# The feed-forward layer's small steps, one step later in a latent-attention loop, and queued behind a copy on VectorE

## The chip, the cores and the metric

The kernel runs on one core of one Trainium2 chip. The metric is the device time of one execution in microseconds. Of several executions the median counts: 2151.29 us before the change, over three runs (2148.95 to 2156.46).

On this core five engines work in parallel, each on its own queue of instructions, in the order in which they stand there: TensorE (PE in the profile) multiplies and transposes, VectorE (DVE) and ScalarE (ACT) do elementwise work and copies, GpSimd (POOL) does some elementwise work as well, SyncE (SP) starts transfers. An engine that waits for another's result holds up everything behind it on its own queue.

## The reference

x holds four sequences of 512 rows and 256 columns. A layer is four parts, each added to x; the first layer is latent attention, feed-forward, cosine attention, the same feed-forward again:

```
x = x + latent_attention(layernorm(x))
x = x + ffn(layernorm(x))
x = x + cosine_attention(layernorm(x))
x = x + ffn(layernorm(x))
```

The second layer has parts of other kinds (a gated linear attention, attention with low-rank adapters, a workspace). The change lies where the feed-forward part behind the latent attention overlaps with that attention. That part is

```
out    = (layernorm(x) @ weight) * scale
v_norm = max(norm(out), 1e-7)                   # one number for each row
out    = out * tanh(v_norm) / (v_norm + 1e-7)
o_norm = max(norm(out), 1e-7)
out    = out * min(0.99 / o_norm, 1)
```

So behind one matrix product there is a chain of operations on one number for each row (in the kernel, tiles of 128x4), and at the end one scaled addition to x. The latent attention is causal attention with 16 heads: scores = q k, softmax, probabilities times values, with rotated parts of q and k, and keys and values read through a low-rank projection.

## The kernel before, in words

x stays in the on-chip memory, one tile of 128x4x256 for each of the four sequences ("batches" b = 0 to 3): 512 rows, in four row tiles (i = 0 to 3) of 128.

The latent attention (`mla`) is one loop over steps n = 32 b + 4 g + i: batch b, pair of heads g (0 to 7), row tile i. A step issues, in this order: the scores of step n (`scores`, L390), the queries of the next pair where i = 0 (`queries`, matmuls at L238, in the loop's helper), parts of the next batch's preparation (`prepare`) (in steps 17, 19, 21 and 23 of 32), the turning of the probabilities of step n - 2 (`turn`, transposes at L417), the values of a finished pair (`values`, L429), and last the feed-forward work that is woven in at this step.

On the other engines this means, for one step: VectorE masks the scores and takes the negated row maximum (L256, `masked`, two instructions on 128 x up to 512, each with a short read of its accumulator), ScalarE takes the exponential (L397), VectorE the reciprocal of the row sums (L401), GpSimd multiplies (L402), TensorE transposes (L417), and VectorE and ScalarE in turn copy the turned probabilities from PSUM into `prt` (`evac`: L129 on VectorE, L133 on ScalarE). For the queries VectorE runs two rope products (L320, L321) and a shuffle (L323), GpSimd adds (L324), ScalarE copies the other half (L378). Scores, turned probabilities, queries and the transposes of a layernorm share three PSUM buffers of one kind ("two"). The first part of the preparation is a layernorm: statistics (L178, L179), the reciprocal root in steps L154 to L160 (`rpow`: VectorE, Ln and Exp on ScalarE, VectorE), xn (L208, four of 128x256), eight transposes (L218) and one copy on ScalarE (L219, `own_xt`).

`ffn_steps` (from L481) is a generator for the feed-forward part of one batch. It stops after the layernorm, and after its transposes; then it issues the matmuls (L238), the product with the scale (L497, 128x1024 on VectorE), four Squares with row sums (L500, ScalarE), and the small steps on 128x4: L503, `rpow` (L154 to L160), L505, L507, Tanh on ScalarE (L509), after which the table of logarithms and exponentials is loaded again (L170), L511 to L518, and the four products that add to x (L520, VectorE). The generators of batches 0, 1 and 2 are called in steps 6, 10 and 14 of the next batch, that of batch 3 in the cosine attention behind it, and a second set of the same generators runs later still, for the feed-forward part behind the cosine attention.

The order of TensorE's instructions is the order in which the program issues them (`manual_schedule`). On the other engines a scheduler decides, which plays the program through with estimated times and issues what it takes to be ready first; the program's own order breaks ties and gives the priorities. `issue_after`, which the kernel uses elsewhere (L956), gives the scheduler a further rule: what is issued inside the block stands behind a named instruction where both are on one engine's queue. It adds no wait for another engine.

Of the kernel before, what the change touches and what calls it, by code (L numbers as in the profile page):

```python
# [9 lines left out]
F32 = mybir.dt.float32  # L10
I32 = mybir.dt.int32
U32 = mybir.dt.uint32
AF = mybir.ActivationFunctionType
ALU = mybir.AluOpType
AX = mybir.AxisListType

P = 128
B = 4
T = 512
D = 256  # L20
NI = T // P
# [4 lines left out]
class Model:  # L26
# [21 lines left out]
    def pool(self, name, bufs=1, **kw):  # L48

        return self.tc.tile_pool(name=name, bufs=bufs, reuse_waits="tile", **kw)  # L50
# [73 lines left out]
    def evac(self, out, in_, scale=None):  # L124

        self.n_evac += 1
        if self.n_evac % 2:
            if scale is None:
                self.nc.vector.tensor_copy(out, in_)  # L129
            else:  # L130
                self.nc.vector.tensor_scalar_mul(out, in_, scale)
        elif scale is None:
            self.nc.scalar.copy(out, in_)  # L133
        else:
            self.nc.scalar.mul(out, in_, scale)
# [342 lines left out]
                    next(woven[n], None)  # L478


    def ffn_steps(self, b, pause=True):  # L481
        nc = self.nc
        w, s = self.ffn_w, self.ffn_s
        eps = 1e-7
        xn, xt = self.norm_tiles()
        self.layernorm(xn, self.x[b])
        p2 = self.norm
        if pause:
            yield
        self.turned(xn, xt)  # L490
        yield
        py = self.two().rearrange("p a (i d) -> p (a i) d", d=D)
        for i in range(NI):
            self.mm(py[:, i, :], [(xt[:, c, i * P : (i + 1) * P], w[:, c, :]) for c in range(NC)])
        y = p2.tile([P, NI, D], F32, name="fy", tag="fy")
        ss = self.small.tile([P, NI], F32, name="f_ss", tag="f_ss")
        nc.vector.tensor_tensor(y, py, s.unsqueeze(1).to_broadcast([P, NI, D]), op=ALU.mult)  # L497
        for i in range(NI):
            sq = p2.tile([P, D], F32, name="fsq", tag="fsq")
            nc.scalar.activation(sq, y[:, i, :], AF.Square, accum_out=ss[:, i : i + 1])  # L500

        n = self.small.tile([P, NI], F32, name="f_n", tag="f_n")
        nc.vector.tensor_scalar_max(ss, ss, 1e-30)  # L503
        self.rpow(n, ss, 1.0, 0.0, self.tmps())
        nc.vector.tensor_tensor(n, n, ss, op=ALU.mult)  # L505
        v = self.small.tile([P, NI], F32, name="f_v", tag="f_v")
        nc.vector.tensor_scalar_max(v, n, eps)  # L507
        f = self.small.tile([P, NI], F32, name="f_f", tag="f_f")
        nc.scalar.activation(f, v, AF.Tanh)  # L509
        self.logs()  # L510
        nc.vector.tensor_scalar_add(v, v, eps)  # L511
        nc.vector.reciprocal(v, v)
        nc.vector.tensor_tensor(f, f, v, op=ALU.mult)
        nc.vector.tensor_tensor(n, n, f, op=ALU.mult)
        nc.vector.tensor_scalar_max(n, n, eps)
        nc.vector.reciprocal(n, n)
        nc.vector.tensor_scalar(n, n, 0.99, 1.0, op0=ALU.mult, op1=ALU.min)
        nc.vector.tensor_tensor(f, f, n, op=ALU.mult)  # L518
        for i in range(NI):
            nc.vector.scalar_tensor_tensor(  # L520
                self.x[b][:, i, :], y[:, i, :], f[:, i : i + 1], self.x[b][:, i, :], op0=ALU.mult, op1=ALU.add
            )
        yield

    @staticmethod
# [1128 lines left out]
def emit(tc, aps):  # L1654


    with ExitStack() as ctx:
        m = Model(ctx, tc, aps)
        ctx.enter_context(tc.manual_schedule(engines={mybir.EngineType.PE}))
        pool = m.pool  # L1660
        sb = ctx.enter_context(pool("shared_b"))
        with m.norms("norm_1", xn=1, xt=1), ExitStack() as stack:
            sa = stack.enter_context(pool("shared_a"))
            with m.psum("ps_1", two=3, acc=2):

                def shared(tag):

                    kb = int(tag.strip("sab"))
                    t = (sa if kb == 16 else sb).tile([P, kb * 256], F32, name=tag, tag=tag)
                    return [t, 0]  # L1670

                ffn = [m.ffn_steps(b) for b in range(B)]
                woven = {32 * (b + 1) + n: ffn[b] for b in range(B - 1) for n in (6, 10, 14)}
                m.mla(shared, woven | {116: m.cos_first()})
                cos = m.cos_load(shared)
                gla = m.gla_load(shared)
                woven = {(0, k): ffn[B - 1] for k in range(3)}
                ffn = [m.ffn_steps(b) for b in range(B)]
                woven |= {(4 * b + 5, k): ffn[b] for b in range(B - 1) for k in (1, 2, 3)}
                prepare, run = m.gla_stage(gla)  # L1680

                def first():

                    m.gla_fold(gla)
                    yield
                    place = shared("s16a")
                    for part in (0, 1, 3, 4, 2):
                        prepare(0, part, place)
                        if part == 1:
                            with m.tc.high_priority(offset=2000):  # L1690
                                prepare(1, "norm", None)
                        if part != 3:
                            yield

                g = first()
                woven |= {at: g for at in ((15, 0), (15, 1), (15, 3), (16, 1), (16, 2))}
                m.cos(cos, woven)
            wp = ctx.enter_context(pool("late_w", side="right"))
            ws = m.ws_load(wp)
            with m.psum("ps_g", st=2, two=1, acc=2), pool("gla_w") as gp, pool("gla_3", 2) as g3, pool(  # L1700
                "gla_2", 2
            ) as g2:
                fold = m.ws_fold(ws, wp, gp)
                extra = {n: [ffn[B - 1]] for n in (1, 3, 5)} | {n: [fold] for n in (6, 9, 10, 13, 14, 15)}
                run(range(B), extra, g2, g3)
        lora = m.lora_load(wp, [shared("s8"), shared("s4a"), shared("s4b")])
        with pool("lora_1", side="right") as l1, pool("lora_w", 2) as lw, m.norms("norm_2", xn=1, xt=2):
            first, run = m.lora_stage(lora, range(B), m.lora_tiles(l1), lw)
            with m.psum("ps_2", two=2, acc=4):
                g = first()  # L1710
                m.ws(ws, ("by", "xt", "xf"), {(1, n): g for n in (1, 2, 4, 8)})
            with m.psum("ps_3", two=4), pool("lora_2", 2) as l2:
                run(l2)
        with m.psum("ps_4", two=2, acc=4):
            m.ws(ws, ("xf", "xt", "by"))
        m.store()
# [121 lines left out]
```

## Time and profile before

| | |
|---|---|
| median of three runs | 2151.29 us |
| lowest, highest | 2148.95, 2156.46 us |
| the profiled execution | 2155.31 us, its span 2153.5 us |
| granted TensorE clock, mean | 0.971 |
| TensorE busy | 1988.9 us (92%) |
| VectorE busy | 1268.0 us (59%) |
| ScalarE busy | 761.1 us (35%) |
| GpSimd busy | 577.8 us (27%) |
| latent attention | about the first 600 us of the span |
| product with the scale (L497) in it | at 229.07, 370.72 and 512.37 us |

The profile is of one execution. A busy engine is one that runs an instruction; idle time of an engine that nothing waits for costs nothing. The profile names, for each wait, the instruction that came last. The three places at which the changed part of the feed-forward layer runs follow each other at 141.65 us. The granted clock is the share of full speed at which TensorE runs; it is 1 or 0.5 at any moment, so the mean says how long it was halved.

### The profile page before, as it was taken

How to read it: one execution, taken by the hardware profiler on the slowest of the kernel's cores; microseconds unless marked ns; L12 is line 12 of the kernel's file. 1: busy time of each engine (PE TensorE's matmuls, PEld its weight loads, DVE VectorE, ACT ScalarE, POOL GpSimd, SP SyncE). 2: the span in 40 equal slices, each digit the busy share in tenths (PEclk: the TensorE clock that was granted, in tenths of full speed). 3: DMA queues.
4: the chain of work that ended last, by engine and by line, in shares of the span. 5: the costliest groups of instructions: out<-in, count | busy, mean ns of one | idle time of the engine just before them, and what ended most of it. 6: DMA issues, size and time to landing. Idle time of an engine off the chain costs nothing.

```text
span 2153.5 us, 25620 instructions
## 1 busy us (share of the span) xinstructions
PE 1988.9 (92%) x9414; PEld 1062.3 (49%) x9414; DVE 1268.0 (59%) x3185; ACT 761.1 (35%) x1696; POOL 577.8 (27%) x530
## 2 busy tenths in 40 slices
PE   7999999999899999999999999988988989899886
PEld 4546555564454454544454454523355644444454
DVE  5565655656446434653664454398955766656545
ACT  2433443434323222322232223234224334334542
POOL 2433333433302212212212221156720122212100
PEclk9999999999999999999999999988899999999898
DMA  5020000000000000000000000010000000000001
GB/s 177 1 91 1 1 1 1 1 1 1 20 1 0 0 1 0 0 1 0 0 1 0 1 0 0 1 46 0 1 25 1 1 1 1 1 1 1 1 1 40
DMA packets 19837, 22.87 MB, mean 11 GB/s; under 512 B 4832, under 2 KB 17664, under 8 KB 19328
## 3 DMA queue, kind: packets, MB, share of 16 engines
q1 hardware_dynamic: 19712, 21.24, 3.0%
q8 instruction: 74, 1.21, 0.2%
q14 instruction: 51, 0.42, 0.1%
HBM read 19.14 MB, written 2.10 MB: 10 GB/s over the span
## 4 chain that ended last, share of the span: by engine, by line
PE 62%; DVE 16%; issue 11%; ACT 6%; POOL 4%; DMA 1%; SPq 0%; POOLq 0%; DVEq 0%; ACTq 0%
PE ps_two L238 26%; PE ps_acc L238 11%; PE ps_two L390 5%; PE ps_acc L429 3%; PE ps_two L1508 3%; DVE ps_two L256 3%; PE ps_two L417 2%; POOL e L687 2%; PE ps_two L1551 2%; DVE gs L888 2%; PE ps_acc L1249 1%; PE ps_two L654 1%; DVE ln_st L178 1%; ACT prob L397 1%; PE ps_acc L645 1%
## 5 line engine op out<-in xcount | busy, mean ns | idle before, releaser
L687 POOL TENSOR_TENSOR e<-e 128x1024 f32<-128x1024 f32 x64 | 150.7, 2355 | 619.4 <-ACT e L679 592.2
L256 DVE CUSTOM_DVE_ANT_0 ps_two<-ps_two,mask 128x256 f32<-128x256 f32 (+3 forms) x512 | 249.7, 503 | 74.3 <-PE ps_two L390 40.7
L679 ACT ACTIVATE e<-ps_two 128x1024 f32<-128x1024 f32 x128 | 130.8, 1023 | 346.8 <-PE ps_two L238 346.6
L238 PE MATMUL ps_acc<-e,cv 128*128 128x512 f32 x512 | 234.9, 601 | 1.4 <-DVE cot L685 0.9
L402 POOL TENSOR_TENSOR prob<-prob,psum_row 128x256 f32<-128x256 f32 (+3 forms) x128 | 159.7, 1255 | 284.6 <-DVE psum_row L401 278.4
L238 PE MATMUL ps_two<-cq,ckt 128*128 128x512 f32 x512 | 230.5, 593 | 3.0 <-DVE cq L656 3.0
L397 ACT ACTIVATE prob<-ps_two,nmax 128x128 f32<-128x128 f32 (+3 forms) x256 | 132.5, 526 | 148.6 <-DVE nmax L256 139.4
L238 PEld LDWEIGHTS ps_acc<-e,cv 128*128 128x128 f32 x512 | 93.5, 190 | 138.3 <-issue 116.0
L238 PEld LDWEIGHTS ps_two<-cq,ckt 128*128 128x128 f32 x512 | 96.6, 190 | 116.9 <-issue 114.8
L238 PE MATMUL ps_two<-own_xt,s 128*128 128x512 f32 x200 | 108.7, 675 | 13.9 <-DVE prt L129 11.1
L238 PE MATMUL ps_two<-own_xt,s16a 128*128 128x512 f32 x256 | 114.9, 592 | 0.1
L238 PE MATMUL ps_two<-s16b,cot 128*128 128x256 f32 x512 | 113.1, 379 | 0.0
L1540 ACT ACTIVATE lo_ex<-ps_two 128x1024 f32<-128x1024 f32 (+3 forms) x128 | 85.3, 704 | 72.8 <-PE ps_two L1508 67.5
L390 PE MATMUL ps_two<-kvt,qx 64*128 64x256 f32 (+3 forms) x512 | 103.6, 481 | 6.1 <-ACT qx L378 2.4
L417 PEld LDWEIGHTS ps_two<-ident,prob 128*128 128x128 f32 x640 | 71.0, 142 | 74.6 <-issue 48.5
L417 PE MATMUL ps_two<-ident,prob 128*128 128x128 f32 x640 | 94.6, 279 | 14.0 <-ACT qx L378 4.5
L238 PEld LDWEIGHTS ps_two<-s16b,cot 128*128 128x128 f32 x512 | 97.3, 190 | 20.1 <-issue 7.7
L1541 POOL TENSOR_SCALAR_AFFINE_SELECT lo_ex<-lo_ex 128x256 f32<-128x256 f32 x128 | 51.7, 408 | 193.5 <-ACT lo_ex L1540 192.3
L688 DVE TENSOR_TENSOR es<-e 128x512 f32<-128x512 f32 x64 | 43.9, 687 | 95.0 <-POOL e L687 93.9
L390 PE MATMUL ps_two<-kpe,qy 64*128 64x256 f32 (+3 forms) x512 | 90.5, 430 | 0.9 <-POOL qy L324 0.9
L1508 PE MATMUL ps_two<-lo_qm,lo_t 32*128 32x128 f32 (+3 forms) x512 | 76.2, 475 | 11.6 <-ACT lo_ex L1540 5.3
L429 PE MATMUL ps_acc<-prt,kv 128*64 128x256 f32 (+3 forms) x512 | 79.0, 452 | 2.7 <-DVE prt L129 2.7
(429 smaller groups left out, 3400.9 us busy)
## 6 DMA issues: line engine op xcount, KB each, us to landing
x<-in_x SPq DMA_DIRECT2D x4, 512.0 KB, 7.7
s16b<-in_mla_wo SPq DMA_DIRECT2D x1, 2048.0 KB, 18.6
s16a<-in_cos_wq SPq DMA_DIRECT2D x1, 2048.0 KB, 9.3
s16b<-in_cos_wo SPq DMA_DIRECT2D x1, 2048.0 KB, 8.6
out_x<-x SPq DMA_DIRECT2D x4, 512.0 KB, 2.9
s16a<-in_mla_wqn SPq DMA_DIRECT2D x1, 1536.0 KB, 13.6
s<-in_mla_wqa SPq DMA_DIRECT2D x1, 1024.0 KB, 10.4
s4a<-in_mla_wkb SPq DMA_DIRECT2D x1, 512.0 KB, 7.4
```

The lines of the kernel that those rows point to most:

```text
L238: self.nc.tensor.matmul(out, lhsT=l, rhs=r, start=k == 0, stop=k == n - 1)
L256: self.nc.vector.tensor_tensor_reduce(out=sc[:, :n], in0=sc[:, :n], in1=self.mask[:, T - n :], scale=-1.0, scalar=3.0e38, op0=ALU.add, op1 ...
L390: nc.tensor.matmul(sc[:, k, :n], lhsT=q[r, rows], rhs=key[r, :n], start=first, stop=not first)
L397: nc.scalar.activation(pr[:, k, :n], sc[:, k, :n], AF.Exp, bias=nm[:, k : k + 1], scale=-1.0, accum_out=sm[:, k : k + 1],)
L402: nc.gpsimd.tensor_tensor(pr[:, :, :n], pr[:, :, :n], sm.unsqueeze(2).to_broadcast([P, 2, n]), op=ALU.mult)
L417: nc.tensor.transpose(pt[:, k, keys], pr[:, k, keys], self.ident)
L429: nc.tensor.matmul(po[k * R : (k + 1) * R, j * P :], lhsT=s.kv[:, j, 0, :], rhs=prt[:, k, j, j * P :], start=j == 0, stop=j == NI - 1,)
L679: nc.scalar.activation(t.e[:, pair * 2 : pair * 2 + 2, :], sc, AF.Exp)
L687: nc.gpsimd.tensor_tensor(e2, t.e[:, 0:2, :], t.e[:, 2:4, :], op=ALU.add)
L1508: nc.tensor.matmul(scs[k // 2][:, k % 2, : keys], lhsT=left[r, rows], rhs=right[r], start=True, stop=True)
L1540: nc.scalar.activation(ex[:, hs, :], sc[:, :, :n], AF.Exp, scale=0.25)
L1541: nc.gpsimd.affine_select(out=ex[:, hs, :P], in_=ex[:, hs, :P], compare_op=ALU.is_ge, fill=0.0, base=0, pattern=[[0, 2], [1, P]], channel_ ...
```

## The change

`evac` keeps the instruction of its latest copy on VectorE. `ffn_steps` takes a further argument, `late`. Where it is set, the generator stops once more behind the four Squares; the small steps are issued at its next call, inside `issue_after` with that latest copy, so that those of them that run on VectorE are queued behind it. `late` is set for batches 0, 1 and 2 of the first set, and their generators are called in step 15 as well. The latest copy at that moment is that of the turned probabilities of step 13. All other uses of the generator stay as they are. No instruction is added or left out. In the changed kernel the small steps L503 to L520 stand at L507 to L524, four lines further down (L501 on).

```diff
@@ evac
             if scale is None:
-                self.nc.vector.tensor_copy(out, in_)
+                self.copied = self.nc.vector.tensor_copy(out, in_)
@@ ffn_steps
-    def ffn_steps(self, b, pause=True):
+    def ffn_steps(self, b, pause=True, late=False):
...
             nc.scalar.activation(sq, y[:, i, :], AF.Square, accum_out=ss[:, i : i + 1])
-
-        n = self.small.tile([P, NI], F32, name="f_n", tag="f_n")
-        nc.vector.tensor_scalar_max(ss, ss, 1e-30)
-        self.rpow(n, ss, 1.0, 0.0, self.tmps())
...
+        if late:
+
+            yield
+        with self.tc.issue_after(self.copied.ins) if late else ExitStack():
+
+            n = self.small.tile([P, NI], F32, name="f_n", tag="f_n")
+            nc.vector.tensor_scalar_max(ss, ss, 1e-30)
+            self.rpow(n, ss, 1.0, 0.0, self.tmps())
+            nc.vector.tensor_tensor(n, n, ss, op=ALU.mult)
...
+            nc.scalar.activation(f, v, AF.Tanh)
+            self.logs()
...
+            for i in range(NI):
+                nc.vector.scalar_tensor_tensor(
+                    self.x[b][:, i, :], y[:, i, :], f[:, i : i + 1], self.x[b][:, i, :], op0=ALU.mult, op1=ALU.add
+                )
         yield
@@ emit
-                ffn = [m.ffn_steps(b) for b in range(B)]
-                woven = {32 * (b + 1) + n: ffn[b] for b in range(B - 1) for n in (6, 10, 14)}
+                ffn = [m.ffn_steps(b, late=b < B - 1) for b in range(B)]
+                woven = {32 * (b + 1) + n: ffn[b] for b in range(B - 1) for n in (6, 10, 14, 15)}
```

More of the change, by code (lines that the diff above doesn't have):

```diff
@@ L500, in ffn_steps @@
             nc.scalar.activation(sq, y[:, i, :], AF.Square, accum_out=ss[:, i : i + 1])
-        n = self.small.tile([P, NI], F32, name="f_n", tag="f_n")
-        nc.vector.tensor_scalar_max(ss, ss, 1e-30)
-        self.rpow(n, ss, 1.0, 0.0, self.tmps())
[L505 to L522, printed above, removed]
+        if late:
+            yield
@@ new lines, in ffn_steps @@
+        with self.tc.issue_after(self.copied.ins) if late else ExitStack():
[3 more added lines that the diff above has]
+            nc.vector.tensor_tensor(n, n, ss, op=ALU.mult)
+            v = self.small.tile([P, NI], F32, name="f_v", tag="f_v")
+            nc.vector.tensor_scalar_max(v, n, eps)
+            f = self.small.tile([P, NI], F32, name="f_f", tag="f_f")
+            nc.scalar.activation(f, v, AF.Tanh)
+            self.logs()
+            nc.vector.tensor_scalar_add(v, v, eps)
+            nc.vector.reciprocal(v, v)
+            nc.vector.tensor_tensor(f, f, v, op=ALU.mult)
+            nc.vector.tensor_tensor(n, n, f, op=ALU.mult)
+            nc.vector.tensor_scalar_max(n, n, eps)
+            nc.vector.reciprocal(n, n)
+            nc.vector.tensor_scalar(n, n, 0.99, 1.0, op0=ALU.mult, op1=ALU.min)
+            nc.vector.tensor_tensor(f, f, n, op=ALU.mult)
+            for i in range(NI):
+                nc.vector.scalar_tensor_tensor(
+                    self.x[b][:, i, :], y[:, i, :], f[:, i : i + 1], self.x[b][:, i, :], op0=ALU.mult, op1=ALU.add
+                )
```

## The prediction

> **What bounds the kernel now.** I read the page first: whole span, busy times, chain that ended last.
>
> ```profile
> span 2153.5 us, 25620 instructions
> PE 1988.9 (92%) x9414; PEld 1062.3 (49%) x9414; DVE 1268.0 (59%) x3185; ACT 761.1 (35%) x1696; POOL 577.8 (27%) x530
> PE 62%; DVE 16%; issue 11%; ACT 6%; POOL 4%; DMA 1%; SPq 0%; POOLq 0%; DVEq 0%; ACTq 0%
> ```
>
> TensorE is busy 92% of the span, so a change on VectorE can win only where TensorE stands still. The sum below is made against this execution: 2155.31 us, 1.8 us more than its span, and 4.0 us above the median of the runs, 2151.29. Next I asked for TensorE's waits around the first of the three places that the change touches (225 to 262 us), and for the clock of four stretches of it.
>
> ```profile
> PE ps_two L238 <- DVE prt L129: 2.0, 1, 2.0
> PE ps_acc L429 <- DVE prt L129: 1.0, 1, 1.0
> ```
>
> ```profile
> 227.47:230.88 3.41, 3.41 (x16) 1.72 (x14) 1.23 (x1) 0.52 (x3) 0.54 (x1) 1.00 0.00 0
> 230.88:234.29 3.41, 1.40 (x15) 1.04 (x13) 1.76 (x9) 2.06 (x10) 0.00 (x0) 1.00 0.00 0
> 234.29:237.71 3.42, 3.42 (x4) 1.36 (x5) 3.10 (x18) 2.37 (x9) 0.31 (x1) 0.50 0.01 2
> ```
>
> The columns are the stretch, its length, the busy time of TensorE, its weight loads, VectorE, ScalarE and GpSimd, the granted clock, DMA. The queries' matmuls (L238) wait 2.0 us for the copy of turned probabilities, the values (L429) 1.0 us for a later one. A stretch in which TensorE was busy 1.40 of 3.41 us is followed by one at half clock. At the second place the stretch from 374.24 us was busy 1.81 of 3.41 us, and the clock stayed full. Then VectorE and GpSimd in order of time.
>
> ```profile
> 229.07 1.23 DVE L497 TENSOR_TENSOR fy<-ps_two,r_ffn_s 128x1024 f32<-128x1024 f32 x1 [2.68 <-PE ps_two L238]
> 232.50 0.17 DVE L503 TENSOR_SCALAR f_ss<-f_ss 128x4 f32<-128x4 f32 x1 [2.20 <-ACT fsq L500]
> ...
> 233.46 0.68 DVE L129 COPY prt<-ps_two 128x512 f32<-128x512 f32 x1
> ...
> 242.44 0.93 DVE L518 TENSOR_TENSOR f_f<-f_f,f_n 128x4 f32<-128x4 f32 x1
> ...
> 245.22 1.21 DVE L129 COPY prt<-ps_two 128x1024 f32<-128x1024 f32 x1
> ```
>
> ```profile
> 242.08 1.27 POOL L324 TENSOR_TENSOR qy<-rope,rope 128x512 f32<-128x512 f32 x1 [2.22 <-DVE f_n L516]
> ...
> 254.33 1.89 POOL L402 TENSOR_TENSOR prob<-prob,psum_row 128x1024 f32<-128x1024 f32 x1 [3.44 <-DVE psum_row L401]
> ```
>
> ```profile
> 254.99 1.26 DVE L157 TENSOR_TENSOR rp<-rp,kvrs 128x4 f32<-128x4 f32 x1
> ```
>
> VectorE stands 2.20 us because L503 waits for the fourth Square; the mask and the copy that the queries need are behind it. That is the stall the change goes for. The other thing to see: L157 on 128x4 takes 1.26 us where GpSimd is inside a normalisation (L402), and both end together (256.25 and 256.22); elsewhere this form takes 0.16. L518 (0.93, else 0.16) ends at 243.37 with GpSimd's L324 (243.35). [...] The masks, rope and copies, which read PSUM, are not held.
>
> **The change, part by part.** Nothing is added or taken away: TensorE, GpSimd and SyncE keep their order, and no DMA moves. On VectorE and ScalarE only the three places in the latent attention move (fy at 229.07, 370.72 and 512.37); swaps of 0.1 to 0.2 us instructions in the last stage I cost at nothing, as they are neighbours in the same wait.
>
> *The wait that goes.* Scores 15 end at 230.95. One mask takes 0.61 until its successor starts, the copy 0.68: the queries can start at 232.3 instead of 234.20, 1.9 us earlier at each place. Queries 8 x 0.43 = 3.44, turn 0.66, scores 1.06: TensorE is through at 237.5.
>
> *The wait that comes.* In the new order the masks of both steps, both pairs of exponentials and the reciprocals (L401) stand ahead of L157, which they start GpSimd's normalisation before. On ScalarE: exponentials of 512 from 233.4 (1.45), Ln pair 0.2, exponentials of 128 (0.8), Exp pair 0.2: L157 can start at 235.95. GpSimd has had its reciprocal since 235.1 and runs 1.89 + 0.61 us, to 237.1 and 237.7. L157 is held to 237.1 (+1.1), L158 to 237.7 (+0.4); unheld they would take 0.15 each, and held as in the row above up to 1.26, and I take the rows, as L402 has the same shape in both. Then come rope's two (0.61 each), small ones, the shuffle (0.73), and only then the four xn (L208), the first done at 240.2. The second meets GpSimd's L324 (1.27, from 240.0) and is held to 241.4 (+0.9), the fourth ends at 242.1; before it ended at 237.18. TensorE, which next needs xn for its transposes (L218), stands from 237.5 to 240.2, 2.7 us, and is then fed one at a time to 242.9 (before 242.3). So the 1.9 us are gone again; the new wait takes their place.
>
> *Behind it.* ScalarE's Tanh waits for L507 (241.5) and reloads its table (1.28) before it copies own_xt, done at 244.4 (243.4): scores 18 at 244.5, +1.0. The copy that the values need no longer stands behind the four L520: values at 246.1, -0.4. But L520 now starts inside a normalisation (1.04 us, held 0.7) and stands ahead of the next masks of 384: these start at 249.0 instead of 246.43. Their exponentials, normalisation and turn are that much later; TensorE has scores and a key projection meanwhile, and loses 0.9 us at the next queries (before 253.97) and some at the turns after. Net +1.0 a place, against about -2.3 if the 2.4 us of holds ahead of xn were not there.
>
> *Third place.* The same start, but the layernorm of the next stage is woven in: its four second xn (4 x 0.33) and the L520 now stand ahead of the masks of step 19, so turn 18 comes after 539.19. And the copy for turn 15 waits behind the last statistics: turn 16 stands some 3 us. Net +1.2.
>
> *Clock.* The trace has no row of the new waits' clock. Lower bound: nothing, +3.2 in all. Upper: each new stretch with TensorE busy under 0.41 is followed by 3.41 us at half clock, up to 1.7 us. I take the rows' side: the stretch from 237.7 would be busy about a tenth, so 241.1 to 244.5 runs at half, doubling 1.7 us of transposes, half of which lies under the wait for own_xt: +0.9; second place +0.6; third, where the values and scores (2.4 and 1.0 us) fall into it, +1.5. The half-clock stretches of before, at places one and three, go, but cost nothing: the second place, without one, reaches its values at the same distance (388.12 less 141.65 is 246.47, against 246.49).
>
> [...]
>
> Sum: 1.0 + 1.0 + 1.2 = 3.2, and 0.9 + 0.6 + 1.5 = 3.0: +6.2 us, 2161.5 against this execution, 2157.5 against the median.
>
> [...]
>
> **Rivals.** *Faster:* the new holds don't come. If GpSimd starts its normalisation after L157 and L158 (0.3 us of work), xn is done 2.4 us sooner, TensorE hardly stands, and each place gains 2.3: -7, 2144. For it: L157 with f_n was not held in before (0.15). Against: there GpSimd was idle until 237.40. It decides once L157 and L158 start under 0.2 us after the reciprocal; I have 0.9.
>
> *No change to be measured:* the waits come, the clock stays: +3.2, 2154.5. For it: before, a half-clock stretch cost nothing at two places.
>
> *Much slower:* the masks 2.6 us late pass on whole, as there are three PSUM buffers for scores, turns and queries, and a full half-clock stretch (1.7) joins: 4.3 x 3 = +12.9, 2164. Against: TensorE has 3.7 us of work in between (scores 1.94, key projection 1.76), and its waits behind them were 0.2 us at most.
>
> **How the numbers follow.** 0.3% (6.45 us) is about what a measurement of this kernel can tell. Chances: the forecast 0.48, over the bound 0.28 of it; clock stays 0.17 (slower 0.02); faster rival 0.15, of which 0.10 over the bound, since -7 is hardly beyond it; much slower 0.20. Faster 0.10, same 0.40, slower 0.50. The range leaves out the faster rival's far end and what lies above +12.9 plus 2 us of spread: 2146 to 2166. The forecast's own is 2153 to 2161.
>
> **What would show it.** Right: no wait of the queries' L238 at the three places; L157 with f_n near 1.2 us; a wait of L218 of 2 to 3 us; half clock within 4 us behind it. Wrong: L157 at 0.16, or values more than 2 us earlier. It would be wrong above all if ScalarE runs the Exp pair ahead of the exponentials of 128, or GpSimd starts later than 235.9.

## The result and the profile after

The change makes the kernel slightly slower: 2158.46 us against 2150.22 us, medians of 22 runs each on the same chips. The ratio is 1.0031, with a 95% interval of 1.0019 to 1.0042. By the ratio that is 6.7 us (4.1 to 9.0); the medians themselves are 8.24 us apart. The forecast was 2157.5 us from a sum of +6.2.

The profiled execution of the changed kernel took 2163.61 us, 8.3 more than that of before. The page of it, span, busy times and chain:

```profile
span 2161.8 us, 25624 instructions
PE 1996.3 (92%) x9414; PEld 1068.4 (49%) x9414; DVE 1274.5 (59%) x3185; ACT 760.1 (35%) x1696; POOL 577.0 (27%) x530
PE 62%; DVE 17%; issue 11%; ACT 5%; POOL 4%; DMA 1%; SPq 0%; POOLq 0%; DVEq 0%; ACTq 0%
```

Every engine runs as many instructions as before (the 4 more of the whole count are on none of these five rows). TensorE runs the same 9414 matmuls and is busy 7.4 us longer, at a mean granted clock of 0.967 in place of 0.971. TensorE's waits at the first place (222 to 262 us) in the changed kernel:

```profile
PE ps_two L218 <- DVE xn L208: 3.5, 2, 2.6
PE ps_two L238 <- ACT prob L397: 1.0, 1, 1.0
PE ps_two L238 <- DVE prt L129: 0.2, 1, 0.2
```

The wait of the queries for the copy has gone from 2.0 to 0.2 us, and that of the values (1.0) is gone as well. In their place the layernorm's transposes (L218) wait 3.5 us in two pieces, and the next queries wait 1.0 us for a late exponential instead of 0.2. VectorE, in order of time, at that place:

```profile
229.51 1.22 DVE L497 TENSOR_TENSOR fy<-ps_two,r_ffn_s 128x1024 f32<-128x1024 f32 x1 [2.68 <-PE ps_two L238]
...
236.38 1.24 DVE L157 TENSOR_TENSOR rp<-rp,f_n 128x4 f32<-128x4 f32 x1
237.54 0.15 DVE L157 TENSOR_TENSOR rp<-rp,ln_rstd 128x4 f32<-128x4 f32 x1
237.66 0.54 DVE L158 SCALAR_TENSOR_TENSOR rp<-rp,f_n 128x4 f32<-128x4 f32 x1
...
240.28 1.66 DVE L208 TENSOR_SCALAR xn<-x,ln_mv,ln_rstd 128x256 f32<-128x256 f32 x2
241.86 0.16 DVE L511 TENSOR_SCALAR f_v<-f_n 128x4 f32<-128x4 f32 x1
241.93 0.72 DVE L208 TENSOR_SCALAR xn<-x,ln_mv,ln_rstd 128x256 f32<-128x256 f32 x2
...
247.33 1.01 DVE L522 TENSOR_TENSOR f_f<-f_f,f_n 128x4 f32<-128x4 f32 x1
248.38 1.67 DVE L524 SCALAR_TENSOR_TENSOR x<-fy,f_f,x 128x256 f32<-128x256 f32 x4
249.97 0.56 DVE L256 CUSTOM_DVE_ANT_0 ps_two<-ps_two,mask 128x384 f32<-128x384 f32 x1
```

For comparison, L157 and the first mask of 384 in the kernel before:

```profile
234.06 0.15 DVE L157 TENSOR_TENSOR rp<-rp,f_n 128x4 f32<-128x4 f32 x1
...
246.43 0.54 DVE L256 CUSTOM_DVE_ANT_0 ps_two<-ps_two,mask 128x384 f32<-128x384 f32 x1
```

And GpSimd in the changed kernel:

```profile
235.71 2.46 POOL L402 TENSOR_TENSOR prob<-prob,psum_row 128x1024 f32<-128x1024 f32 x2 [7.28 <-DVE psum_row L401]
240.52 1.27 POOL L324 TENSOR_TENSOR qy<-rope,rope 128x512 f32<-128x512 f32 x1 [2.35 <-DVE rope L323]
```

L157 and L158 run inside the two normalisations and end with them (the second L402 and the L158 end at 238.17 and 238.20). The two xn of one row take 1.66 us where the next two take 0.72: the second of them ends 0.15 us behind GpSimd's L324. L524 stands ahead of the masks of 384, which start 20.46 us after fy instead of 17.36.

What it did to TensorE's clock, in three stretches of the same place (stretch, length, busy time of TensorE, weight loads, VectorE, ScalarE, GpSimd, granted clock, DMA):

```profile
238.97:242.38 3.41, 0.63 (x2) 0.28 (x2) 3.41 (x11) 2.18 (x4) 1.27 (x1) 1.00 0.00 0
242.38:245.79 3.41, 3.40 (x16) 2.93 (x16) 1.72 (x11) 2.90 (x5) 0.00 (x0) 0.50 0.00 0
245.79:249.20 3.41, 3.41 (x20) 1.50 (x22) 3.34 (x8) 0.59 (x3) 1.04 (x1) 1.00 0.02 5
```

The stretch with the wait is followed by one at half clock, in which the transposes and the turns take about twice as long (L218: 2.04 us for the last seven, where all eight took 1.09 before; L417: 1.91 us for eight, 1.04 before).

The third place looks different. TensorE's longest waits there (505 to 545 us) before:

```profile
PE ps_two L238 <- DVE prt L129: 2.0, 1, 2.0
PE ps_two L390 <- ACT prob L397: 1.9, 1, 1.9
PE ps_two L417 <- DVE prt L129: 0.8, 1, 0.8
```

The longest in the changed kernel, and the clock of the stretches that matter:

```profile
PE ps_two L417 <- DVE prt L129: 3.5, 1, 3.5
PE ps_two L417 <- ACT prob L397: 2.0, 1, 2.0
PE ps_two L390 <- ACT qx L378: 1.0, 1, 1.0
```

```profile
529.13:532.54 3.41, 0.93 (x6) 0.51 (x8) 3.41 (x15) 1.19 (x3) 0.00 (x0) 1.00 0.00 0
532.54:535.95 3.41, 3.41 (x18) 1.33 (x14) 2.35 (x12) 2.34 (x10) 1.04 (x1) 0.50 0.00 0
...
542.78:546.19 3.41, 1.45 (x13) 1.21 (x14) 1.49 (x8) 2.14 (x8) 1.12 (x1) 1.00 0.00 0
546.19:549.60 3.41, 2.85 (x16) 1.82 (x12) 3.04 (x9) 0.58 (x1) 2.44 (x3) 0.50 0.00 0
549.60:553.02 3.42, 3.42 (x12) 1.42 (x12) 0.67 (x3) 1.93 (x5) 1.21 (x2) 0.50 0.02 5
```

The turn of step 16 waits 3.5 us, that of step 18 another 2.0, and each wait is followed by half clock, the second time over two stretches.

To see what a place costs I measure, in each trace, from the start of the product with the scale (fy) to the first matmul of the values (L429), for the pair then finished and for the next pair. These distances need no comparison of whole runs:

| kernel | place 1 | place 2 | place 3 | fy of place 1 to last values |
|---|---|---|---|---|
| before | 17.41 / 34.90 | 17.41 / 34.89 | 15.90 / 32.05 | 355.88 |
| after | 18.08 / 36.38 | 18.20 / 36.38 | 16.17 / 37.24 | 362.83 |

At the next pair the change costs 1.5, 1.5 and 5.2 us. The two attentions differ by 6.95 us and not by their sum of 8.2, since in the profile of before the pair behind that next one took 17.22 us, where it took 16.08 in the changed kernel and 16.10 in the first experiment, whose order is that of before; I have not followed up why. The start (fy 0.44 later) and the rest of the span (0.9 longer) make up the remainder of the 8.3.

### The profile page after: what moved, and what is told of

It is laid out like the page before. It is cut to its first block, busy times and chain, and to the rows that moved or that the text cites. A ratio compares the mean times of both kernels' runs of the same rounds, so it can differ in the third digit from the quotient of the medians.

```text
span 2161.8 us, 25624 instructions
## 1 busy us (share of the span) xinstructions
PE 1996.3 (92%) x9414; PEld 1068.4 (49%) x9414; DVE 1274.5 (59%) x3185; ACT 760.1 (35%) x1696; POOL 577.0 (27%) x530
## 4 chain that ended last, share of the span: by engine, by line
PE 62%; DVE 17%; issue 11%; ACT 5%; POOL 4%; DMA 1%; SPq 0%; POOLq 0%; DVEq 0%; ACTq 0%
PE ps_two L238 25%; PE ps_acc L238 11%; PE ps_two L390 5%; PE ps_two L1512 3%; PE ps_acc L429 3%; DVE ps_two L256 3%; PE ps_two L417 3%; POOL e L691 2%; DVE gs L892 2%; PE ps_two L1555 2%; PE ps_acc L1253 1%; DVE ln_st L178 1%; ACT prob L397 1%; PE ps_two L658 1%; DVE ps_st L889 1%
## 5 line engine op out<-in xcount | busy, mean ns | idle before, releaser
L402 POOL TENSOR_TENSOR prob<-prob,psum_row 128x256 f32<-128x256 f32 (+3 forms) x128 | 159.6, 1255 | 291.0 <-DVE psum_row L401 279.0
L417 PE MATMUL ps_two<-ident,prob 128*128 128x128 f32 x640 | 97.6, 285 | 17.2 <-ACT prob L397 4.8
L417 PEld LDWEIGHTS ps_two<-ident,prob 128*128 128x128 f32 x640 | 73.4, 145 | 78.6 <-issue 52.7
L238 PE MATMUL ps_two<-own_xt,s 128*128 128x512 f32 x200 | 102.2, 640 | 10.0 <-DVE prt L129 5.2
L401 DVE RECIPROCAL psum_row<-psum_row 128x2 f32<-128x2 f32 x128 | 21.1, 165 | 104.8 <-ACT prob L397 98.0
```

The source lines that it names most:

```text
L238: self.nc.tensor.matmul(out, lhsT=l, rhs=r, start=k == 0, stop=k == n - 1)
L402: nc.gpsimd.tensor_tensor(pr[:, :, :n], pr[:, :, :n], sm.unsqueeze(2).to_broadcast([P, 2, n]), op=ALU.mult)
L417: nc.tensor.transpose(pt[:, k, keys], pr[:, k, keys], self.ident)
```

## The experiments

The theory was that of the prediction: the small steps, once behind the copy, fall into GpSimd's normalisations, are held, and drag the layernorm of the next batch with them; TensorE then stands, and its clock is halved behind that. The rivals: the extra stop or the rule alone cost time; the late addition (L524) is what counts; the clock costs nothing, as the prediction had found at two places of before. All ratios are to the kernel before on the same chip, with 95% intervals.

### The extra stop alone

The generator stops once more and is called in step 15, but nothing is queued behind the copy (against before):

```diff
+        if late:
+            yield
...
-                woven = {32 * (b + 1) + n: ffn[b] for b in range(B - 1) for n in (6, 10, 14)}
+                woven = {32 * (b + 1) + n: ffn[b] for b in range(B - 1) for n in (6, 10, 14, 15)}
```

> Only the extra stop is kept: the small steps are issued in step 15, but not queued behind the copy. Theory (the loss comes from the order on VectorE alone): VectorE's order at the three places is that of before, since the scheduler still finds the Squares' sums first, so the waits are those of before: 2.0 us at the queries, none at L218, time within 2 us of before (ratio 0.999 to 1.001). Rival (one step later is itself too late): values about 1 us later at each place, +3 to +6 us.

Measured: 0.9995 [0.9979, 1.0011]; distances 17.42 / 34.90, 17.41 / 34.89, 15.85 / 32.00. TensorE's waits at the first place in this kernel:

```profile
PE ps_two L238 <- DVE prt L129: 2.0, 1, 2.0
PE ps_acc L429 <- DVE prt L129: 1.0, 1, 1.0
```

They are those of before. Issuing the small steps later changes nothing by itself: the scheduler still finds them ready and takes them first, and the order on all engines is that of before. The rule without the stop was not run.

### The holds taken away

L402 is left out in steps 15 and 16 of batches 1 to 3, in the changed kernel and, as a control, in the kernel before:

```diff
-                nc.gpsimd.tensor_tensor(
-                    pr[:, :, :n], pr[:, :, :n], sm.unsqueeze(2).to_broadcast([P, 2, n]), op=ALU.mult
-                )
+                if b == 0 or 4 * g + i not in (15, 16):
+                    nc.gpsimd.tensor_tensor(
+                        pr[:, :, :n], pr[:, :, :n], sm.unsqueeze(2).to_broadcast([P, 2, n]), op=ALU.mult
+                    )
```

> The changed kernel without GpSimd's normalisation (L402) in steps 15 and 16 of batches 1 to 3; the probabilities of these six steps stay unnormalised, all else is the same, and so is the order on VectorE. Theory (L157 and L158 are held by that normalisation): L157 with f_n takes 0.15 us instead of 1.24, L158 0.15 instead of 0.54; the first xn starts about 1.5 us sooner after fy; TensorE's wait before L218 falls from 3.5 to about 2 us; the second xn is still held by the sum of rope (L324). Each place gains 1 to 2 us on the changed kernel, 3 to 6 in all: +0 to +3 us over before. Rival (the order alone makes xn late, and the long L157 is only waiting): L157 stays near 1 us or xn does not move, +8 us over before as in the changed kernel.

> The same normalisations left out of the kernel before, as the control. Theory: they lie off the path there (the turn of step 15 comes 3 us after its normalisation has ended), time within 2 us of before. Rival: they are on the path, 2 us or more faster, and the run before it would show nothing of the hold.

Measured: 1.0004 [0.9986, 1.0022] for the changed kernel without these normalisations, 0.9995 [0.9975, 1.0015] for the control. VectorE in the former, and its TensorE wait:

```profile
236.20 0.16 DVE L157 TENSOR_TENSOR rp<-rp,f_n 128x4 f32<-128x4 f32 x1
...
238.64 1.67 DVE L208 TENSOR_SCALAR xn<-x,ln_mv,ln_rstd 128x256 f32<-128x256 f32 x2
```

```profile
PE ps_two L218 <- DVE xn L208: 2.0, 2, 1.2
```

Without L402 beside it L157 takes 0.16 us instead of 1.24, and xn starts 9.32 us after fy instead of 10.77: 1.45 us, by the 1.1 and 0.4 that the prediction gave to the two holds. L324 is still there, and the two xn still take 1.67 us: the second ends 0.15 us behind it (240.31 and 240.16). Distances: 15.54 / 33.51, 17.16 / 34.71, 14.72 / 33.81; those of the control are 17.16 / 34.64, 17.31 / 34.80, 15.73 / 31.95. So the first values come 2.5 us sooner than in the changed kernel at the first place, but only 1.0 at the second and 1.5 at the third. At the first place no half clock is left behind the shorter wait (the eight turns behind it take 1.04 us, as before), at the second, where the wait is 2.4 us in two pieces, one stretch of it remains. So the holds are a cause, and without them the change would be a gain at the next pair of 1.4 us at the first place and of 0.2 at the second, against before; for the whole run it comes out even, because the late turns of the third place stay (33.81 for the next pair, 32.05 before).

### The clock kept up

TensorE gets dummy products to do where it would stand. The last addition (L524) is issued in step 17, behind the latest copy on VectorE, where it stands in the changed kernel, so that the extra products don't move it (against after; `keep` multiplies the mask by the identity, and nothing reads the product):

```diff
+                    xn, s.xt = self.norm_tiles(p2)
+                    self.layernorm(xn, self.x[b])
+                    if b > 0:
+                        self.keep(5)
+                    self.turned(xn, s.xt)
...
+                if n == 32 * 3 + 18:
+                    self.keep(7)
...
+        if late:
+            yield
+        with self.tc.issue_after(self.copied.ins) if late else ExitStack():
             for i in range(NI):
...
-                woven = {32 * (b + 1) + n: ffn[b] for b in range(B - 1) for n in (6, 10, 14, 15)}
+                woven = {32 * (b + 1) + n: ffn[b] for b in range(B - 1) for n in (6, 10, 14, 15, 17)}
```

> The changed kernel with TensorE kept busy in its new waits by products that nobody reads: five 128x512 products (5 x 0.43 us) ahead of the transposes L218 at places one and two, seven ahead of turn 16 at place three; the additions to x (L524) are pinned behind the copy of turn 15, where they stand in the changed kernel. Theory (stretches in which TensorE is nearly idle are followed by half clock): no half clock behind the waits, L218's and the next transposes at 0.11 us each instead of 0.22, values about 0.7 us sooner after fy at places one and two, 1.5 at place three: 2 to 4 us less than the changed kernel. Rival (the half clock is absorbed as it was in before): the clock stays full and the values come no sooner, within 1 us of the changed kernel.

Measured: TensorE at the first place, and the clock:

```profile
241.45 4.56 PE L244 MATMUL ps_acc<-mask,ident 128*128 128x512 f32 x10
245.85 1.04 PE L218 MATMUL ps_two<-ident,xn 128*128 128x128 f32 x8
```

```profile
241.80:245.20 3.40, 3.40 (x9) 1.52 (x8) 3.40 (x9) 1.87 (x2) 1.27 (x1) 1.00 0.00 0
245.20:248.60 3.40, 3.09 (x22) 2.22 (x22) 2.85 (x18) 3.09 (x7) 0.17 (x1) 1.00 0.00 0
```

No half clock is left in any of the three places. Distances: 17.11 / 34.59, 17.12 / 34.60, 18.68 / 33.67. The next pairs came at 36.38, 36.38 and 37.24 us in the changed kernel: 1.8, 1.8 and 3.6 us less. Against before (34.90, 34.89, 32.05), -0.3, -0.3 and +1.6 are left.

These differences are the worth of the half clock only roughly. The extra products take 4.56 us and, at the third place, 6.28 us, where the waits were 3.5, so TensorE starts later than its inputs allow (the first values of the third place come 2.5 us later than in the changed kernel, where 1.5 sooner was expected). And two copies have changed their place in the order: that of own_xt stands behind two exponentials, and at the third place that of a finished pair's values (`ot`) stands behind the late addition (L524) instead of ahead of it, so that the masks of step 19 come 1.0 us sooner. So the 3.6 us of the third place are not clock alone.

The time, 1.0027 [1.0004, 1.0050], shows no gain. One set of extra products stands in batch 0 too, where nothing is late, and fy of the first place comes 3.3 us later; and behind the last values this kernel needs 1575.6 us, the changed one 1569.4, before 1568.5. VectorE, ScalarE and GpSimd have another order in a later stage, between about 1405 and 1440 us, but the matmuls behind it are still level with those of the changed kernel (within 0.2 us near 1440 us). The loss comes later: 2.6 us until about 1530 us, and 5.6 between 1573 and 1613 us, where this trace has 6.8 us of half clock and that of the changed kernel none. Why the clock differs there is not shown.

### Two places only

The change is made in batches 0 and 1 alone (against after):

```diff
-                ffn = [m.ffn_steps(b, late=b < B - 1) for b in range(B)]
+                ffn = [m.ffn_steps(b, late=b < B - 2) for b in range(B)]
```

> The change at places one and two alone; the third has the order of before again. From the changed kernel's trace (values of the next pair after fy 36.38 us against 34.90 at places one and two, 37.2 against 32.0 at the third): +3.0 us over before, 5 us less than the changed kernel, ratio to before near 1.0014. Rival (all three places lose alike, and the third only looks worse): +5.5 us, ratio 1.0026.

Measured: 1.0032 [1.0022, 1.0042], as much as with all three; the expectation missed. Distances: 19.38 / 36.86, 19.25 / 36.74, 15.82 / 31.99. The third place is back to that of before, but the two others cost 1.9 us each, not 1.5. At the marks that is 3.8 us; the ratio stands for 6.9, and the rest is not accounted for. The waits and the order at these places are those of the changed kernel; the clock isn't:

```profile
237.19:240.60 3.41, 0.32 (x3) 0.14 (x1) 3.41 (x11) 1.87 (x2) 1.07 (x1) 1.00 0.00 0
240.60:244.02 3.42, 3.02 (x13) 2.67 (x14) 2.51 (x13) 2.42 (x4) 0.20 (x1) 0.50 0.00 0
244.02:247.43 3.41, 3.41 (x12) 1.52 (x10) 2.56 (x6) 1.01 (x5) 1.04 (x1) 0.50 0.00 0
247.43:250.84 3.41, 3.41 (x24) 1.68 (x24) 3.33 (x9) 0.86 (x3) 0.00 (x0) 1.00 0.02 5
```

Half clock lasts two stretches here, 6.8 us, where the profile of the changed kernel has one. The work up to there is the same, only 1 us earlier, and it lies otherwise against these stretches of 3.41 us: the wait at 240.1 to 241.0 falls partly into the second, which was busy 3.02 us. The first values then come at 19.4 instead of 18.1 us. That this place against the stretches makes the difference is my estimate from these two profiles. They show that the time of one place, from one profile, is uncertain by 1 to 2 us.

### The late addition moved back

The four products that add to x are queued behind the masks of step 18 instead (against after; `masked` keeps its latest instruction as `mask_op`):

```diff
+        if late:
+            yield
+        with self.tc.issue_after(self.mask_op.ins) if late else ExitStack():
             for i in range(NI):
...
-                woven = {32 * (b + 1) + n: ffn[b] for b in range(B - 1) for n in (6, 10, 14, 15)}
+                woven = {32 * (b + 1) + n: ffn[b] for b in range(B - 1) for n in (6, 10, 14, 15, 18)}
```

> The changed kernel, but the four additions to x (L524) are issued in step 18 and queued behind that step's masks of 384. Nothing else moves on any engine. Theory (L524 ahead of those masks makes the next queries late): the first values come as in the changed kernel (18.1 us after fy), the masks of 384 about 2 us sooner, TensorE's wait for the exponentials ahead of the next queries (1.0 us) goes, the next values come 36.4 - 1.0 = 35.4 us after fy; 2 us less than the changed kernel in all, as at the third place nothing is changed. Rival (the queries were late through half clock alone): 36.4 as before, no change.

Measured: 1.0029 [1.0013, 1.0045]; the 2 us less than the changed kernel did not show. Distances: 19.19 / 36.67, 19.15 / 36.63, 16.43 / 35.55. The wait of the next queries for the exponentials falls from 1.0 to 0.2 us. But here too half clock covers two stretches at each place (at the first, a granted clock of 0.50 and 0.51 from 240.4 to 247.2 us). From the first values to the next it is 17.5 us, against 18.3 in the changed kernel, but the kernel with two places has 17.5 as well without this edit, and 0.2 us for that wait. So it can't be told apart: the term of 0.9 us in the prediction may be real behind one stretch of half clock and covered behind two. The third place, whose order this edit leaves as it is, shows how much the clock does: its next pair comes 1.7 us sooner than in the changed kernel (35.55 instead of 37.24), and the second half clock of that place, from 546.19 us in the changed kernel, is not there.

### The layernorm ahead of the small steps

If xn is what is late, it can be made in step 13, when VectorE has time. The loop in which it stands then allows the next stage's first part to start at step 109 instead of 116 (against after):

```diff
-                    s.xt = self.normed(b, p2)
+                    if b == 0:
+                        s.xn, s.xt = self.norm_tiles(p2)
+                        self.layernorm(s.xn, self.x[b])
+                    self.turned(s.xn, s.xt)
...
+                if n < len(steps) and b + 1 < B and 4 * g + i == 13:
+                    ns = seqs[b + 1]
+                    ns.xn, ns.xt = self.norm_tiles(p2)
+                    self.layernorm(ns.xn, self.x[b + 1])
...
-                m.mla(shared, woven | {116: m.cos_first()})
+                m.mla(shared, woven | {109: m.cos_first()})
```

> The change, with the layernorm of the next batch issued in step 13 instead of 17 (its transposes stay in step 17), and the first two layernorms of the cosine attention in step 109 instead of 116. Theory (the change loses because xn, on the same queue, is dragged behind the small steps, rope and GpSimd): L157 may still be held, but xn is done long before; no wait of L218 for xn, no half clock behind it; queries 1.9 us sooner as in the changed kernel, first values 15 to 16 us after fy (17.4 before, 18.1 changed): 4 to 7 us less than before, ratio 0.997 to 0.998. Rival (the new wait only passes to the next thing late, the copy of own_xt behind the Tanh's table loads): first values near 17.4, within 1.5 us of before.

Measured: 1.0007 [0.9995, 1.0019]; distances 17.88 / 35.61, 16.92 / 35.61, 15.12 / 31.14. TensorE's longest waits and ScalarE, first place:

```profile
PE ps_two L393 <- ACT own_xt L219: 2.7, 1, 2.7
PE ps_two L420 <- ACT qx L381: 1.2, 1, 1.2
```

```profile
239.55 1.28 ACT L520 ACT_TABLE_LOAD   x1
240.85 0.21 ACT L520 ACTIVATE f_f<-f_v 128x4 f32<-128x4 f32 x1
241.07 1.28 ACT L170 ACT_TABLE_LOAD   x1
242.36 1.01 ACT L219 COPY own_xt<-ps_two 128x1024 f32<-128x1024 f32 x1
```

The wait for xn is gone, and the next one takes over: the copy of the transposes stands on ScalarE behind Tanh and its two table loads, and half clock follows that wait as well (243.75 to 247.16 us). So the gain that was expected did not come; the rival held. The third place is 0.9 us better than before. With the addition moved back as well (both edits together) it is the same within the measurement:

> Both of the last two edits together. Theory: 0.5 to 1 us a place less than with the early layernorm alone, 5 to 9 us less than before, ratio 0.996 to 0.9975. Rival: the additions to x are covered once TensorE has no gap ahead of them, as with the early layernorm alone.

Measured: 1.0006 [0.9995, 1.0017], the same two waits of 2.7 and 1.2 us; distances 16.94 / 35.62, 18.16 / 36.71, 15.12 / 31.15. In all stages behind the last values the two kernels have the same order on every engine, yet in the two profiles that part takes 1572.0 and 1564.9 us. So single profiles differ there by 7 us through something other than the order; the second has 13.4 us less of half clock in it (mean granted clock 0.974 against 0.971).

### The table loads taken away

Tanh is written with the exponential, so that the two table loads of 1.28 us are not made (the form holds while exp(2v) stays in range):

```diff
-            nc.scalar.activation(f, v, AF.Tanh)
-            self.logs()
+            nc.scalar.activation(f, v, AF.Exp, scale=2.0)
             nc.vector.tensor_scalar_add(v, v, eps)
+            nc.vector.scalar_tensor_tensor(v, f, 1.0, v, op0=ALU.add, op1=ALU.mult)
             nc.vector.reciprocal(v, v)
-            nc.vector.tensor_tensor(f, f, v, op=ALU.mult)
+            nc.vector.scalar_tensor_tensor(f, f, -1.0, v, op0=ALU.add, op1=ALU.mult)
```

This was done in all eight uses of the generator, in the kernel before, in the changed kernel, and in the changed kernel with the early layernorm and the addition moved back:

> The kernel before, with tanh(v) / (v + eps) worked out as (exp(2v) - 1) / ((exp(2v) + 1) (v + eps)) in all eight uses, so that ScalarE loads no table for it (two loads of 1.28 us fall away at each use) and VectorE has one more small step. Theory (in the old order the loads lie beside the queries, which run at the same time): 0 to 1 us a place, 1 to 4 us less than before in all, ratio 0.998 to 1.000. Rival (the loads are on the path everywhere, 2.5 us at each of eight uses): 10 us or more less.

> The changed kernel with the same arithmetic for tanh. Theory (the held small steps make xn late, and the loads come on top of it only at the copy of own_xt): the wait of L218 for xn stays at 3.5 us and the half clock with it; the copy of own_xt starts with the end of the transposes as it did, so the values are 0 to 0.5 us sooner at places one and two, and at the third, where the copy of turn 15 waits behind the statistics, 0 to 1: +4 to +8 us over before, ratio 1.002 to 1.004. Rival (the loads make the loss): back to within 2 us of before.

> The change with the early layernorms, with the additions to x behind the masks of step 18, and with the arithmetic for tanh. Theory (with xn early the last late thing was the copy of own_xt behind the two loads: TensorE waited 2.7 us for it, and 1.2 us for the copy of qx's buffer): that wait goes, first values 14 to 15.5 us after fy at places one and two (17.4 before), no half clock behind it; 6 to 12 us less than before, ratio 0.9945 to 0.997. Rival (one more wait takes its place): within 3 us of the kernel before with the same arithmetic.

Measured: 1.0022 [1.0004, 1.0039] for before, 1.0059 [1.0039, 1.0078] for the changed kernel, 1.0003 [0.9990, 1.0017] for all edits together; none of the three came out as expected in total. Distances: 17.82 / 35.31, 17.23 / 34.71, 15.05 / 29.64 for before, 17.78 / 36.35, 17.91 / 36.48, 16.31 / 35.40 for the changed kernel (four runs only), 14.57 / 32.28, 14.56 / 32.27, 14.35 / 28.68 for all edits. In the changed kernel L218 still waits 3.5 us for xn: the loads weren't what came last there. With xn early they are: the values of the first place come 3.3 us sooner than with the early layernorm alone, and from fy of the first place to the last values it takes 349.34 us, 6.5 less than before (and 3.7 less than with the extra stop alone, 353.05). Yet the total is no better, since the rest takes 1572.7 us (before 1568.5). The other two of these kernels lose there too: 1572.4 and 1571.3 us. The other five uses of the generator lie in later stages, in which VectorE, ScalarE and GpSimd then have another order. How that costs time is not shown: up to 1385 us, with four of the five uses done, the matmuls of the rest are level with those of before within 0.1 us; the loss comes behind that.

So the last run makes the exponential form only where `late` is set, with all else as in the kernel with all edits (against that one):

```diff
-            nc.scalar.activation(f, v, AF.Exp, scale=2.0)
+            if late:
+                nc.scalar.activation(f, v, AF.Exp, scale=2.0)
...
+            else:
+                nc.scalar.activation(f, v, AF.Tanh)
+                self.logs()
...
```

> The last kernel, but with the arithmetic for tanh at the three late places alone; the five uses in later stages load the table as before, so that the order in the gated linear attention is that of before. Theory (the 3 to 4 us that the latent attention gained were lost again where the order of the later stages had changed): first values again 14.6 us after fy, the latent attention 3 to 8 us shorter than before, the rest as before: 3 to 7 us less than before, ratio 0.9967 to 0.9986. Rival (a gain of this size in one stage is lost anyway in how the clock's windows fall in the later ones): ratio 0.999 to 1.001.

Measured: **0.9963 [0.9946, 0.9980]**, 2144.39 against 2155.05 us, faster than before, where the changed kernel was slower. TensorE's waits at the first place, the longest at the third, and the clock at the first:

```profile
PE ps_two L420 <- ACT f_f L521: 1.2, 1, 1.2
PE ps_two L420 <- ACT prob L400: 0.5, 1, 0.5
PE ps_two L238 <- ACT prob L400: 0.4, 1, 0.4
PE ps_two L238 <- DVE prt L129: 0.2, 1, 0.2
```

```profile
PE ps_two L420 <- ACT prob L400: 1.6, 1, 1.6
```

```profile
238.10:241.50 3.40, 2.21 (x17) 1.57 (x17) 3.38 (x13) 1.59 (x3) 1.27 (x1) 1.00 0.00 0
```

No wait is longer than 1.2 us at the first two places and 1.6 at the third, and the clock stays whole at all three. Next pairs come at 32.27, 32.27 and 28.68 us, 2.6, 2.6 and 3.4 sooner than before; from fy of the first place to the last values it takes 346.1 us (355.88 before, 353.05 with the extra stop alone), the rest 1568.0. Whether the early layernorm and the other arithmetic would have brought this without the change itself was not run.

## Why the prediction was right, point by point

The direction and nearly the size came out: +6.2 predicted, +8.24 measured, inside the range (2146 to 2166) and the forecast's own (2153 to 2161). The path is the one that was forecast: the queue on VectorE, the holds, xn late, half clock behind it. That the sum came so near is in part luck, as two of its terms were off in opposite ways. Its steps:

- *The wait that goes.* Right. The queries start 3.28 us after fy, 5.13 before: 1.85 us sooner, where 1.9 was said. The wait is 0.2 at all three places.
- *The wait that comes.* Right in place and size. L157 was to end with GpSimd's first normalisation (+1.1): 1.24 us instead of 0.16. L158 (+0.4): 0.54. The second xn held by L324 (+0.9): 1.66 us for two instead of 0.72. L218 waits 2.6 and 0.9 us, where 2.7 and then a feed one at a time was said. The experiment without L402 shows the cause of the first two. That L324 holds xn rests on the ends of the two instructions; it wasn't taken away. No row of before shows the 0.9 us of that hold: the one xn in its first 600 us that began inside a GpSimd instruction (at 19.07 us) took 0.49 us, the others 0.41. In the changed kernel the xn beside L324 took 1.35.
- *Behind it.* The own_xt copy ends 15.57 us after fy, 14.32 before: +1.25, where +1.0 was said, clock included. The reason was another: the copy was said to stand behind the table loads of Tanh, but the second load ends at 243.56 us, and the copy starts at 244.07, when the transposes, at half clock, have ended (244.04). The addition ahead of the masks, said to make them 2.6 us late, makes them 3.1 late, and the next queries lose 0.8 us where 0.9 was said. That this wait decides is not shown (0.2 us in the kernel with two places).
- *The net of a place without the clock: mis-sized.* +1.0, +1.0 and +1.2 were taken, in sum 3.2. With the clock kept up it is -0.3, -0.3 and +1.6, in sum 1.0, by an experiment that also moved two copies. The terms above were nearly right one by one; at places 1 and 2 their net was not. It may be that TensorE's work covers more of the late own_xt copy and of the late masks than the sum allowed; that was not separated.
- *Clock: mis-sized the other way.* +0.9, +0.6 and +1.5, in sum 3.0, were taken; 1.8, 1.8 and 3.6 came out, in sum 7.2, the last of them not of the clock alone. The half-clock stretch came where it was expected, within 4 us behind the wait, and over the values and scores at the third place. It followed stretches that were busy 0.63, 0.93 and 1.45 of 3.41 us, and 0.32 in the kernel with two places. Two things were missing: half of it was to lie under the wait for own_xt, but that copy waited for the slowed transposes; and at the third place a second wait, that of turn 18, was followed by half clock over two stretches. The two errors offset each other in part: 1.0 + 7.2 is 8.2, the sum at the marks, against 6.2.
- *Third place.* Predicted +2.7 in all, measured +5.2: the turn of step 16 stands 3.5 us (some 3 were said), turn 18 comes 2.2 us late, and the second half clock adds the rest. In the kernel with the late addition moved, whose order at this place is the same, the second half clock is not there, and the place costs +3.5.
- *The rivals.* "Faster" would have needed L157 within 0.2 us of the first reciprocal (L401); it starts 0.8 us behind its end, and 0.67 us after GpSimd has begun. "Clock stays" was ruled out by the half-clock stretches. "Much slower", the late masks passing on whole, didn't come at places 1 and 2; the third place, at +5.2, is of that size.

## What to carry to other kernels

Moving small work behind something urgent on one queue moves everything that depends on it: ask which instruction is the next that TensorE needs, and what the other engines do at the time at which the small work now runs. L157, on 512 numbers, took 1.24 us here instead of 0.15, and ended with GpSimd's L402 beside it. The wait that is taken away uncovers the next, here the copy, then xn, then the table loads; the one kernel with a measured gain had all three gone and the later stages left alone. And a change in one stage is best measured by its own marks, since the rest of this program took 1564.9 or 1572.0 us in two profiles with one and the same order, which is as much as the change itself.

## What the runs showed of the hardware

- Half clock came without an idle stretch ahead of it. In the profiles of before and after the granted clock is 1 or 0.5 in every record, and each stay at half lasts 3.41, 6.83, 10.24 or 13.65 us, but for the one that the span's end cuts short. In the latent attention, stretches of 3.41 us in which TensorE was busy 1.40 us (from 230.88 us in before) and 1.45 us (third place of the changed kernel) were followed by half clock; others busy 1.56 us (from 525.71 us in the changed kernel) and 1.81 us (second place of before) were not. A stretch that itself ran at half clock was followed by another when it was busy 3.02 us (with two places), 2.85 us (from 546.19 us in the changed kernel) or even 3.41 us (from 1401.66 us in before), and not when it was busy 3.09 us (from 1740.86 us in the changed kernel) or 3.40. In the last stage one busy 2.21 us, from 1966.14 us in the changed kernel, was followed by half clock too. So no single limit on the busy time of a stretch fits, and what sets the clock stays open.
- The changed kernel spreads more from run to run: 2149.95 to 2169.46 us, 19.5 us, against 13.2 for before in as many runs. That the phase of the clock's stretches against the waits makes the difference was not shown run by run. The kernel with two places, where one profile has half clock over two stretches at each, spreads by only 2.8 us in ten runs.
- An instruction on 512 numbers (L157) took 1.24 us beside a GpSimd instruction (L402) and 0.16 us without: it ended with its neighbour, at 237.62 and 237.60 us, so that what it cost here was the remainder of the neighbour's time. The rope products (L320, L321) took 0.67 to 0.69 us in before, in all 72 that stand in the first 600 us, inside a GpSimd instruction or not.
